# A graph-attention kernel: smaller scratch buffers, a carry read where the matmul left it, and the table's first half written in three pieces

## The chip, the cores and the metric

The kernel runs on one core of one Trainium2 chip. The metric is the device time of one execution in microseconds (us). A core has a matrix engine (PE, with its weight loads shown as PEld), a vector engine (DVE), a scalar engine (ACT), a general engine (POOL) and an engine that only issues transfers and waits (SP). Each runs its own instructions in order. They meet through semaphores. Transfers are issued from the queues of SP, ACT and POOL and are carried out by 16 DMA engines that all queues share, in packets. Matmuls write to PSUM, of which one tile in this kernel is a bank of 512 fp32 columns on 128 partitions; DVE and ACT read PSUM and SBUF.

## What is computed

32 graphs, each `x[b]` of 512 channels by 1024 nodes, pass through two layers. Cut to what matters (the weights `wm`, `support` and `kernel` are all `adj`):

```python
# layer 0: attention over the 1024 nodes of a graph
q = einsum('c,bcn->bn', wq, x);  k = einsum('c,bcn->bn', wk, x)
scores = q[:, None, :] + k[:, :, None]                  # row m, column n
scores = where(scores > 0, scores, 0.01 * scores)
att = softmax(scores, axis=-1)
agg = einsum('bcn,bmn->bcm', x, att)
x = layernorm(x + relu(einsum('oc,bcm->bom', adj, agg) + bm[:, None]))
# layer 1
x = layernorm(x + einsum('bnf,nm->bmf', x, adj * adj) + bias)
```

`layernorm` is over the 1024 nodes, with variance plus 1e-5 and no scale or shift.

The kernel never forms the 1024 x 1024 attention. With the nodes sorted by `q` from the largest down, the nodes of a row `m` with a positive score are the first `of[m]` of the order. Their weights are exp(q) times a factor of the row; those of the others are exp(0.01 q) times another. So a running sum from the top ("up") and one from the bottom ("down") of weighted rows `z = adj x`, kept for every place of the order, hold everything: row `m` reads one line of a table, scales its two halves and adds them.

## The kernel before, in words

All inputs and products are fp32. A batch is one graph. Its stages are small Python functions, each of which issues the instructions of one step; a dictionary `ops` gives each a short word. Three lists of such words, written out in full, `head` (line 827), `loop` (line 1026) and `tail` (line 1044), say in which order all instructions of all engines are issued. A word `td.-1.0` is the step `td` for the batch before the current one, argument 0. `head` covers the first 15 batches of starts, `loop` is issued for b = 15 to 22, `tail` drains. In the steady state four batches are in work at once: the products and ranks of batch b, the table of b - 1, the attention's result of b - 2, layer 1 of b - 3. As every engine runs in order, a step that waits holds all later words of its own engine.

The steps in the order of one batch, with their words:

- `ld` (line 98) loads `x[b]`, four transfers of 128 partitions x 4 KB. `pa`, `pc`, `co`, `cc` (lines 234 to 264) compute q and k; `pc` copies from PSUM to the tile `part`. `qw` and `ro` (lines 266 to 276) write q to DRAM and read it back on all partitions into the tile `qb`.
- `rk` (line 294) ranks the nodes on DVE, `ct` (line 311) counts on ACT; both write a throw-away tile.
- `z`, `zU` and their like compute `z` on PE; `zc` and others copy it to `zt`, which has 514 columns (`ZR`): 512 of `z`, a one, and minus q. `sc` (line 438) scatters its rows to DRAM by rank, with POOL, to `sorted_z`.
- `sl` (line 452) loads the sorted rows in two halves of four rows for each partition into the right side of the tile `tab`, which has 8 rows of 2 x 514 columns on each of the 128 partitions. The pool `one` has one buffer for each tag, so there is one `tab` at a time.
- `se` (line 465) takes the exponentials on ACT. `u` (line 475) makes the 8 running sums from the top within a partition, `d` (line 487) those from the bottom.
- `cu` (line 510) carries the sums of the partitions across partitions, a matmul of a triangle of ones (`before`, whose first column is all ones) with the partitions' totals: output partition p is the sum of the partitions in front of p, and output partition 0 is the total of all. `uc` (line 513) copies it to row 0 of `tab`'s left side with a factor per partition, `inner`, which is 0 on partition 0 and 1 elsewhere. `tu` (line 532) adds that row to rows 1 to 7. `te` (line 536) copies the total to a line of its own, in the buffer of the tag `qb`, and `tl` (line 548) writes that line as row 1024 of the table in DRAM.
- `cd` (line 520) does the same from the other side with `behind`, in two matmuls of 257 columns; `dc` (line 523) copies the carry from PSUM to SBUF, into the buffer of the tag `part`, and `td` (line 540) adds it to the right side of `tab`, four rows at a time.
- `tw` (line 543) writes `tab` to the table in DRAM in two halves, each 128 partitions x 4 rows x 1028 columns: 16,448 contiguous bytes for a partition.
- `tb` and `tp` (lines 278 to 292) fetch the largest q. `g` (line 552) gathers the table's rows by `of`, with POOL; `mw`, `ms`, `mx` (lines 561 to 582) scale and add the halves; `t` (line 596) turns the result on PE; `r` (line 605) adds it to x.
- Then layer 1: `s0`, `rt`, `rce`, `n0` normalise; `t1` to `t4`, `U`, `V`, `Y`, `Z`, `11`, `12`, `21` are its products in a scheme of seven multiplications; `up`, `lr`, `ll` add the parts; `s1`, `ra`, `rb`, `r1`, `n` normalise again, and `st` (line 782) writes the output.

Three tags of the pool `one` matter for the change. `part` holds in turn `part`, DVE's throw-away tile of the ranks, and the down carry. `qb` holds `qb` and the line of the total. `tab` is described above. Where two tiles share a tag, the later one's first write waits for the last use of the earlier one.

PSUM has four single banks that `bank` (line 83) hands out and `release` (line 92) takes back; the dictionary `over` says at which word. The two banks of the down carry come back at `dc`.

## Time and profile before

| | |
|---|---|
| median of 3 runs | 1946.24 us (1945.54 to 1951.74) |
| the profiled execution's own time | 1946.45 us |
| its span, first to last instruction | 1944.7 us |
| mean granted PE clock | 0.991 |
| chain that ended last | PE 72%, DMA 8%, DVE 6%, ACT 5%, issue 2% |
| DMA, mean over the span | 287 GB/s; 558.55 MB moved |

Busy time is what an engine spent in instructions; the rest it waited or had nothing to issue. A group's row gives the line, the engine, the operation, output and inputs, shapes, the count, then busy us and mean ns of one, then the idle time of the engine before them with what ended it. A row of waits reads: engine, line, what it waited for, us in total, times, the longest. "SPq" is SP issuing a transfer; the time it shows is that of issuing, not of the transfer. A DMA queue's line gives packets, MB and the packets' time as a share of 16 engines over the span; q1 is SP's queue, q0 POOL's, q10 ACT's.

The times of one period of the steady part can be read from a batch to the next: the first halves of the table go out at 895.0, 952.6, 1010.2, 1067.7 and 1125.4 us.

### The profile page before, as it was taken

The numbers are of one execution on the slowest core, as the hardware profiler recorded it, in microseconds if no ns is written. First come the engines' busy times: TensorE is split into PE (matmuls) and PEld (weight loads), VectorE is DVE, ScalarE is ACT, GpSimd is POOL, SyncE is SP. The second block draws the span as 40 slices with busy tenths as digits, with TensorE's granted clock in tenths as the row PEclk, the third lists the DMA queues.
The fourth block names the chain that finished last, engine by engine and source line by source line (L and its number), as shares of the span: only waits on it lengthen the run. The fifth ranks groups of instructions, "written<-read, shape, count | busy, mean of one in ns | idle before, by whom it ended". The sixth has DMA issues, their size and how long they took to land.

```text
span 1944.7 us, 23294 instructions
## 1 busy us (share of the span) xinstructions
PE 1871.7 (96%) x6947; PEld 1059.4 (54%) x6949; DVE 1699.4 (87%) x2732; ACT 1543.5 (79%) x2791; POOL 863.2 (44%) x1074
## 2 busy tenths in 40 slices
PE   7997999999999999999999999999999999998897
PEld 3653565555555545556555556555565555554343
DVE  5887899999898989989999988998898999988983
ACT  3556878988888878888888888888887888877896
POOL 4243444455444445444445544445444345445340
PEclk9998999999999999999999999999999999999999
DMA  6467888777878777878787888777788677787762
GB/s 247 165 245 287 309 321 321 267 303 286 335 304 300 285 295 282 327 306 311 288 312 282 304 308 306 299 291 283 291 312 330 270 301 280 298 321 302 277 250 86
DMA packets 147577, 558.55 MB, mean 287 GB/s; under 512 B 19662, under 2 KB 19802, under 8 KB 139260
## 3 DMA queue, kind: packets, MB, share of 16 engines
q1 hardware_dynamic: 90080, 354.92, 48.4%
q0 software_dynamic: 57344, 202.15, 27.4%
q8 instruction: 55, 0.90, 0.2%
q14 instruction: 70, 0.57, 0.1%
q10 hardware_dynamic: 28, 0.01, 0.0%
HBM read 287.59 MB, written 269.42 MB: 286 GB/s over the span
## 4 chain that ended last, share of the span: by engine, by line
PE 72%; DMA 8%; DVE 6%; ACT 5%; issue 2%; POOL 1%; SPq 0%; another core or an unknown queue 0%; DVEq 0%; POOLq 0%; ACTq 0%
PE z_ps L339 17%; PE sum_ps L656 17%; PE pair_ps L656 10%; PE z_sum_ps L383 8%; PE z_pair_ps L383 6%; PE pair_ps L708 5%; PE agg_ps L600 4%; DMA tab<-sorted_z 3%; DMA table<-tab 2%; PE qk_ps L240 2%; DMA x<-in_x_dram 1%; DVE tab L530 1%; PE carry_ps_False L501 1%; DMA got<-table,of 1%; PE carry_ps_True L501 1%
## 5 line engine op out<-in xcount | busy, mean ns | idle before, releaser
L556 POOL DMA_INDIRECT got<-table,of x256 | 294.9, 1152 | 536.2 <-DVE junk_v L301 169.9
L339 PE MATMUL z_ps<-adj_t,x 128*128 128x512 f32 x1088 | 487.8, 596 | 5.8 <-ACT part L248 2.7
L444 POOL DMA_INDIRECT sorted_z<-zt,to x256 | 298.5, 1166 | 212.2 <-ACT zt L345 70.5
L301 DVE SCALAR_TENSOR_TENSOR junk_v<-qb,qkc,tie 128x1024 uint8<-128x1024 f32 x256 | 328.8, 1284 | 18.6 <-DMA qb<-q_row 14.7
L339 PEld LDWEIGHTS z_ps<-adj_t,x 128*128 128x128 f32 x1088 | 203.2, 191 | 231.6 <-issue 217.9
L316 ACT ACTIVATE junk_s<-qb,qkc 128x1024 uint8<-128x1024 f32 x256 | 293.5, 1147 | 34.8 <-DMA qb<-q_row 26.4
L656 PE MATMUL sum_ps<-zt,S 128*128 128x512 f32 x512 | 238.0, 596 | 3.3 <-ACT g L700 2.0
L483 DVE SCALAR_TENSOR_TENSOR tab<-tab,ac 128x514 f32<-128x514 f32 x224 | 168.6, 753 | 42.1 <-ACT tab L479 16.5
L576 ACT ACTIVATE got<-got,bd 128x512 f32<-128x512 f32 x256 | 175.2, 718 | 22.9 <-DVE bd L571 16.1
L581 DVE SCALAR_TENSOR_TENSOR got<-got,bd 128x512 f32<-128x512 f32 x256 | 184.6, 745 | 5.9 <-ACT got L576 4.6
L609 DVE SCALAR_TENSOR_TENSOR x<-agg_ps,small,x 128x1024 f32<-128x1024 f32 x128 | 162.6, 1280 | 21.7 <-PE agg_ps L600 21.3
L591 ACT ACTIVATE junk<-g,tv 128x1024 uint8<-128x1024 f32 x128 | 146.6, 1146 | 42.7 <-DVE g L728 31.7
L493 DVE SCALAR_TENSOR_TENSOR tab<-tab,ac 128x513 f32<-128x513 f32 x224 | 167.4, 747 | 3.8 <-ACT junk_s L316 1.4
L759 POOL TENSOR_SCALAR tv<-tv 128x1 f32<-128x1 f32 x124 | 48.8, 393 | 274.1 <-ACT junk L591 267.1
L656 PEld LDWEIGHTS sum_ps<-zt,S 128*128 128x128 f32 x512 | 96.9, 191 | 123.9 <-issue 108.4
L591 ACT ACTIVATE junk<-x,tv 128x1024 uint8<-128x1024 f32 x128 | 146.8, 1147 | 16.6 <-DVE x L609 13.0
L780 ACT ACTIVATE g<-g,nb,tv 128x1024 f32<-128x1024 f32 x124 | 152.3, 1237 | 7.6 <-POOL nb L770 7.6
L530 DVE TENSOR_TENSOR tab<-tab,carry 128x2052 f32<-128x2052 f32 x64 | 145.1, 2290 | 5.3 <-ACT carry L508 5.3
L627 ACT ACTIVATE x<-x,tv 128x1024 f32<-128x1024 f32 x128 | 140.9, 1141 | 0.3
L600 PEld LDWEIGHTS agg_ps<-ident,got 128*128 128x128 f32 x1024 | 116.2, 141 | 34.8 <-issue 22.0
L600 PE MATMUL agg_ps<-ident,got 128*128 128x128 f32 x1024 | 129.7, 274 | 2.6 <-DVE got L581 1.0
L530 DVE TENSOR_TENSOR tab<-tab 128x1539 f32<-128x1539 f32 (+1 forms) x64 | 129.3, 2023 | 0.6 <-ACT tab L516 0.5
(134 smaller groups left out, 3251.2 us busy)
## 6 DMA issues: line engine op xcount, KB each, us to landing
table<-tab SPq DMA_DIRECT2D x64, 2056.0 KB
tab<-sorted_z SPq DMA_DIRECT2D x64, 1028.0 KB
x<-in_x_dram SPq DMA_DIRECT2D x128, 512.0 KB
out_dram<-g SPq DMA_DIRECT2D x128, 512.0 KB
qb<-q_row SPq DMA_DIRECT2D x32, 512.0 KB
sorted_z<-zt,to POOLq DMA_INDIRECT x256
got<-table,of POOLq DMA_INDIRECT x256
adj_in<-in_adj_dram SPq DMA_DIRECT2D x1, 1024.0 KB
```

The costliest lines, as they stand in the source:

```text
L301: nc.vector.scalar_tensor_tensor(s.junk, s.qb, s.q[:, j : j + 1], tie[:, at : at + N], ALU.subtract, ALU.is_gt, accum_out=s.rank[:, j : j ...
L316: nc.scalar.activation(junk, s.qb, AF.Sign, bias=s.k[:, j : j + 1], accum_out=s.sign[:, j : j + 1])
L339: nc.tensor.matmul(s.z[j], xt[:, c, j * P : (j + 1) * P], adj_t[:, c, :], start=(c == 0), stop=(c == CT - 1),)
L383: nc.tensor.matmul(ps, a[:, i, k * P : (k + 1) * P], v[:, i, :], start=start and i == 0 and (k == 0 or bank == 1), stop=(i == 1), skip_gro ...
L444: nc.gpsimd.indirect_dma_start(out=sorted_z[b % 2][:, :], out_offset=bass.IndirectOffsetOnAxis(ap=s.to[:, j : j + 1], axis=0), in_=zt[:, j ...
L530: nc.vector.tensor_tensor(v, v, c, ALU.add)
L556: nc.gpsimd.indirect_dma_start(out=s.got[:, j, :], out_offset=None, in_=table[b % 2][:, :], in_offset=bass.IndirectOffsetOnAxis(ap=s.of[:, ...
L576: nc.scalar.activation(down, down, AF.Copy, scale=s.bd[:, 1, j : j + 1])
L581: nc.vector.scalar_tensor_tensor(up, up, s.bd[:, 0, j : j + 1], down, ALU.mult, ALU.add)
L591: nc.scalar.activation(junk, t, AF.Square, bias=v[0][:, i : i + 1], scale=-float(N), accum_out=v[1][:, i : i + 1],)
L600: nc.tensor.matmul(s.agg[o][:, j * P : (j + 1) * P], s.got[:, j, o * P : (o + 1) * P], ident, is_transpose=True, start=(j % 4 == 0), stop= ...
L656: nc.tensor.matmul(ps, a[:, k, g * P : (g + 1) * P], v[:, k, :], start=False, stop=(k == 1), skip_group_check=True,)
```

## The change

It has five parts.

- The tag `part` shrinks from 514 to 256 columns and holds only `part`; DVE's throw-away tile gets a tag of its own; the line of the total and the carry's copy are gone.
- The down carry stays in PSUM. `cd` makes it in matmuls of 512 and 2 columns, `dc` is gone, and `td` adds it from there: column 512 for all eight rows at once (in the first `td`), columns 0 to 511 for four rows at a time. The two banks come back at the second `td`.
- `uc` copies without the factor `inner`, so that row 0 of `tab`'s left side holds the total on partition 0. `te` is gone, and `tl` writes row 1024 of the table from there. `tu` is as it was, and so adds the total to rows 1 to 7 of partition 0 too.
- The table's row 0 must have zeros on the left: they are written once at the start, and `tw`'s first half leaves them out, so that it is three transfers: partitions 1 to 127; rows 1 to 3 of partition 0; and the right side of row 0.
- All three order lists are new. The loop's words are the same but for `te` and `dc`; 62 of its 196 words stand elsewhere in the order, mostly by a few places. On SP, `tl` moves behind a store and `qw`; on PE, `cd` moves behind `co` and one `t`.

```diff
-    rows = one.tile([P, ZR], F32, tag="part", name="rows")[0 : 3 * CT, 0:P]
+    rows = one.tile([P, Q], F32, tag="part", name="rows")[0 : 3 * CT, 0:P]
...
-    spare, inner = small[0:1, 9:10], small[:, 10:11]
+    spare = small[0:1, 9:10]
...
-    nc.vector.tensor_scalar(inner, ident[:, 0:1], -1.0, 1.0, ALU.mult, ALU.add)
...
     for t in table:
         nc.scalar.dma_start(out=t[N : N + 1, ZR:], in_=zero)
+        nc.scalar.dma_start(out=t[0:1, 0:ZR], in_=zero)
...
-        s.part = one.tile([P, ZR], F32, tag="part", name=f"part_{b}")[:, 0:Q]
+        s.part = one.tile([P, Q], F32, tag="part", name=f"part_{b}")
...
-            s.junk = one.tile([P, 4 * ZR], U8, tag="part", name=f"junk_v_{b}")[:, 0:N]
+            s.junk = one.tile([P, N], U8, tag="junk_v", name=f"junk_v_{b}")
...
     def carry_up_copy(b):
         half = ZR // 2
         for h, t in enumerate(st[b].cup):
-            nc.scalar.activation(
-                st[b].tab[:, 0, h * half : (h + 1) * half], t, AF.Copy, scale=inner
-            )
+            nc.scalar.copy(st[b].tab[:, 0, h * half : (h + 1) * half], t)
 
     def carry_down(b):
-        st[b].cdown = carry(b, behind, st[b].zs[:, 0, :])
-
-    def carry_down_copy(b):
-        st[b].carry = one.tile([P, ZR], F32, tag="part", name=f"carry_{b}")
-        carry_copy(st[b].cdown, st[b].carry)
+        s, v = st[b], st[b].zs[:, 0, :]
+        s.cdown = []
+        for lo, hi in ((0, C), (C, ZR)):
+            t = bank(f"carry_ps_{b}_{lo}", f"carry.{b}.False", whole=False)[:, 0 : hi - lo]
+            nc.tensor.matmul(t, behind, v[:, lo:hi], start=True, stop=True)
+            s.cdown.append(t)
 
     def spread_carry(v, c):
-        n = v.shape[1]
-        c = c[:, 0:D].rearrange("p (o c) -> p o c", o=1).broadcast_to([P, n, D])
+        n, w = v.shape[1], v.shape[2]
+        c = c[:, 0:w].rearrange("p (o c) -> p o c", o=1).broadcast_to([P, n, w])
         nc.vector.tensor_tensor(v, v, c, ALU.add)
...
-    def table_up_end(b):
-        st[b].end = one.tile([P, N], F32, tag="qb", name=f"total_{b}")[0:1, 0:ZR]
-        carry_copy([t[0:1, :] for t in st[b].cup], st[b].end)
-
     def table_down(b, h):
-        spread_carry(st[b].zs[:, 4 * h : 4 * h + 4, 0:D], st[b].carry)
+        s = st[b]
+        if s.carried is None:
+            s.carried = True
+            spread_carry(s.zs[:, :, C:D], s.cdown[1])
+        spread_carry(s.zs[:, 4 * h : 4 * h + 4, 0:C], s.cdown[0])
 
     def table_write(b, h):
         rows = table[b % 2][0:N, :].rearrange("(p j) c -> p j c", j=NT)
         at = slice(4 * h, 4 * h + 4)
-        nc.sync.dma_start(out=rows[:, at, :], in_=st[b].tab[:, at, :])
+        v = st[b].tab
+        if h:
+            nc.sync.dma_start(out=rows[:, at, :], in_=v[:, at, :])
+            return
+        nc.sync.dma_start(out=rows[1:P, at, :], in_=v[1:P, at, :])
+        nc.sync.dma_start(out=rows[0:1, 1:4, :], in_=v[0:1, 1:4, :])
+        nc.sync.dma_start(out=rows[0:1, 0, ZR : 2 * ZR], in_=v[0:1, 0, ZR : 2 * ZR])
 
     def table_last(b):
-        nc.sync.dma_start(out=table[b % 2][N : N + 1, 0:ZR], in_=st[b].end)
+        nc.sync.dma_start(out=table[b % 2][N : N + 1, 0:ZR], in_=st[b].tab[0:1, 0, 0:ZR])
...
-                due[key] = due.get(key, 2 if key.endswith("True") else 1) - 1
+                due[key] = due.get(key, 2 if key.endswith("False") else 1) - 1
```

Of the new lists, the part of `loop` from the last sums to the table's writes:

```diff
-    ls.-3.0 ls.-3.1 d.-1.0 s1.-3.3 tu.-1.0 z.1.2 te.-1 ra.-3.3 s1.-3.2 tl.-1 mx.-2.0 st.-3.1
-    rb.-3.3 tu.-1.1 pc.1 n.-3.0 qw.1 r1.-3.3 t.-2.2 st.-3.0 zc.1.2 ro.1 cd.-1 ra.-3.2 r.-2.2
-    n.-3.3 rb.-3.2 co.1 t.-2.1 r1.-3.2 dc.-1 cc.1 ce.0 st.-3.3 n.-3.2 t.-2.3 tb.0 r.-2.1 z.1.3
-    st.-3.2 td.-1.0 s0.-2.1 ct.1.7 td.-1.1 tw.-1.0
+    ls.-3.0 ls.-3.1 d.-1.0 uc.-1 st.-3.1 s1.-3.3 tu.-1.0 z.1.2 s1.-3.2 ra.-3.3 mx.-2.0 rb.-3.3
+    pc.1 tu.-1.1 n.-3.0 qw.1 r1.-3.3 tl.-1 t.-2.2 zc.1.2 st.-3.0 ro.1 co.1 r.-2.2 t.-2.1
+    ra.-3.2 n.-3.3 rb.-3.2 cd.-1 cc.1 r1.-3.2 ce.0 r.-2.1 n.-3.2 t.-2.3 st.-3.3 tb.0 z.1.3
+    td.-1.0 s0.-2.1 st.-3.2 ct.1.7 td.-1.1 tw.-1.0
```

## The prediction

> **What bounds the kernel now.** I read the page's busy line first, then one period of the steady part, cut at the events around the table.

> ```profile
> span 1944.7 us, 23294 instructions
> ## 1 busy us (share of the span) xinstructions
> PE 1871.7 (96%) x6947; PEld 1059.4 (54%) x6949; DVE 1699.4 (87%) x2732; ACT 1543.5 (79%) x2791; POOL 863.2 (44%) x1074
> ```

> PE leaves 1944.7 - 1871.7 = 73 us, and none of it in the period below. The next view is the timeline of SP, which issues the transfers (start, time of issuing, line, transfer, count):

> ```profile
> 1010.17 2.54 SPq L546 DMA_DIRECT2D table<-tab  x2
> 1021.85 0.92 SPq L463 DMA_DIRECT2D tab<-sorted_z  x2
> 1048.19 1.77 SPq L101 DMA_DIRECT2D x<-in_x_dram  x4
> ...
> 1067.74 2.53 SPq L546 DMA_DIRECT2D table<-tab  x2
> ```

> The two halves of the table go out (L546), the same tile `tab` is reloaded for the next batch (L463) once they have left it, and 57.57 us after one write comes the next. The first exponential on the reload (L468 on ACT) starts at 1029.72. Those three points cut the period; the view of stretches gives each engine's busy time in them:

> ```profile
> core 0: us, PE busy (x) PEld busy (x) DVE busy (x) ACT busy (x) POOL busy (x), PEclk, DMA share, GB/s
> 1010.20:1021.90 11.70, 11.70 (x42) 7.10 (x41) 11.63 (x20) 10.10 (x20) 0.00 (x0) 1.00 0.86 365
> 1021.90:1029.70 7.80, 7.80 (x37) 6.84 (x36) 6.67 (x12) 5.83 (x8) 5.89 (x5) 1.00 0.87 312
> 1029.70:1067.70 38.00, 38.00 (x142) 19.26 (x141) 34.40 (x56) 32.22 (x61) 22.00 (x29) 1.00 0.77 281
> ```

> PE has no gap, so it is the bound; but a loop of events through `tab` (write, reload, exponentials, sums, write) fills the same period with almost no slack. SP's waits say so:

> ```profile
> SPq L463 <- DMA table<-tab: 242.7, 32, 12.0
> SPq L549 <- ACT total L508: 182.0, 21, 30.9
> ```

> Every one of the 32 reloads waits for the table's transfer, 7.6 us each. Whatever lengthens that transfer by more than a few us lengthens every batch. So I looked at its packets. The tile's 64 half writes are 8,192 packets of 16,448 bytes (one row of partition each), median 616 ns, from 611; 10 to 90 in 100 lie at 613 to 636. One half is 128 packets over 16 engines, 8 x 0.616 = 4.93 us; both halves, 9.9 us, took 10.07 to 11.2 us from first to last packet, so an engine sends them one after another.

> How many engines does a transfer get? The page counts packets by queue, and the small queue of ACT can be counted out whole:

> ```profile
> q1 hardware_dynamic: 90080, 354.92, 48.4%
> q0 software_dynamic: 57344, 202.15, 27.4%
> ...
> q10 hardware_dynamic: 28, 0.01, 0.0%
> ```

> ```profile
> table<-zero ACTq DMA_DIRECT2D x2, 2.0 KB
> rows<-in_L_gnn_wq_dram ACTq DMA_DIRECT2D x1, 2.0 KB
> rows<-in_L_gnn_wk_dram ACTq DMA_DIRECT2D x1, 2.0 KB
> rows<-in_L_gnn_bm_dram ACTq DMA_DIRECT2D x1, 2.0 KB
> ```

> q10 carried three loads of four rows and two writes of one row. The trace has 12 data packets of 512 bytes, 2 of 2,056 and 14 of 4 bytes: the last are closing packets, four for each four-row load (12) and one for each one-row write (2). SP's queue q1 closes the same way: its closing packets are 7,360, which is 450 transfers of 128 rows x 16, plus 32 of four rows x 4, plus 32 of one row x 1. So the row count sets the engines, in equal shares: 128 rows 16 engines, 4 rows 4, 1 row 1.

> **The change, part by part.**

> *The first half's write* (`table_write`, h = 0) becomes three transfers: partitions 1 to 127 (127 x 16,448 bytes), rows 1 to 3 of partition 0 (12,336 bytes), and the right half of its row 0 (2,056). No row of the trace has 127 rows. Lower bound: 16 engines with unequal shares, 8 x 0.616 = 4.9 us, as now. Upper bound: equal shares only. 127 has no divisor up to 16 but 1, so one engine sends 127 x 0.616 = 78.2 us. I take the upper value, because every transfer of the trace has equal shares, and a four-row one stays on 4 engines with 12 idle; nothing evens shares out.

> [...]

> Now the loop again, on the engine that has it all. 78.2 (127 rows), 12,336/16,448 x 0.616 = 0.46, a 2,056-byte packet 0.085, and behind them in the same queue the second half's 8 packets, 4.93: 83.7 us. The shortest stretch from first write to reload in the trace is 11.4 us for 9.86 us of packets, so 1.5 us for start and landing: 85.2 us instead of 12.7 (394.0 us over the 31 stretches between batches). That is 31 x 85.2 - 394 = +2,247 us. The last batch's gathers wait for its table as well: 85.2 - 11.5 = +74.

> What is queued behind the wait: on SP the next x load, total, stores and q row; POOL's gathers wait for the same landing, ahead of the next scatters in its list; ACT stops at the exponentials, with a `norm0`, `u`'s scale and all PSUM copies behind them; DVE at the second `u`; PE, after `U` of the first half, at products of rows that ACT has not normalised. Within some 22 us of the write all stand. What each did meanwhile is saved once: reload to exponentials is 203.5 us over 31 (6.6 each), partly ACT's own lateness; the shortest are 5.2 to 5.5, so 5.4 x 31 = 167, -36 us. Exponentials to the next write (1,166 us over 31, 38 each) I keep: DVE is busy 34.4 of 38.0, in order, most of it behind the reload. It could shrink by 5 us (DVE without gaps, less `T1`, done in the wait), or grow: after PE gaps of 4 to 7 us the profile's clock stands at 0.5 for 3.4 or 6.8 us, so up to 3.4 us of PE a batch after a gap this long.

> *Copies off ACT.* The 64 down copies go (21.3 us busy), the 64 of the totals (20.0), and the 64 scaled copies of 467 ns become plain ones, 369 ns in the same shape: 64 x 0.098 = 6.3. Together 47.6 us, 1.5 a batch. ACT is idle 57.5 - 48.15 = 9.4 us of the period above, so this is worth nothing: PE's work covers it now, the wait after; with neither cover it would be 1.5 us a batch.

> *The carry read in PSUM.* DVE's two additions of 2,052 columns (2,290 ns) become two of 2,048 and one of 8 (an 8-column operation takes 169): +0.16 x 32 = 5 us, inside DVE's 3.6 us of gaps a batch. The rows for the source:

> ```profile
> L643 DVE TENSOR_TENSOR zt<-x 128x1024 f32<-128x1024 f32 x32 | 39.1, 1221 | 1.1 <-ACT x L627 0.9
> L426 DVE TENSOR_TENSOR zt<-z_pair_ps,zt 128x1024 f32<-128x1024 f32 x30 | 36.6, 1219 | 6.7 <-issue 3.7 <-PE z_pair_ps L383 2.9
> ```

> With one operand in PSUM 1,219 ns, with both in SBUF 1,221: no price. [...]

> Two PSUM banks stay held until the second addition instead of the copies, some 5.6 us longer (1064.2 to 1069.8 in this period); if a later product wants them, PE waits for DVE, 0 to 5 us.

> *PE.* The carry matmuls become 512 and 2 columns instead of 257 and 257. The columns stay 514, but a weight load (191 ns) no longer hides behind a two-column pass: 0 to 2 x 0.191 = 0.4 us a batch, 0 to 12 us in all; free under the wait.

> *Buffers and lists.* `part` no longer waits for carry and ranks (ACT waited 4.0 us for that), `qb` not for the total (2.7). `tl` moves on SP behind one store and the q row write; it no longer waits for the copies (182 us of SP's waiting, none seen by PE). In the steady list 62 of 196 words stand elsewhere, by a few places. At set-up two 2 KB writes come, one tiny DVE operation goes. All this lies between the 73 us that PE has to give and a few us of new waits; I take 0.

> Sum against the profiled execution (1946.45 us around its span): 1946.45 + 2,247 + 74 - 36 = 4,231, so **4,230 us**; the shown runs' median, 1946.24, is the same to 0.01%. Its own range: 31 x 5 = 155 less, or 31 x 3.4 = 105 (clock), 31 x 2.4 = 74 (reload as late as the 7.8 above) and 35 (packets at their mean of 624) more: 4,075 to 4,445.

> **Rivals.**

> 1. *The 127 rows are spread over all 16 engines*. Then PE remains the bound, and what is left is the head and tail, where the carry is on the path: from its matmul to the addition 3.3 us, of which the copies 0.6 and the wait for them go, some 1.5 us in four or five batches, -7, less buffer waits of 4.0 and 2.7; against it up to 12 us of weight loads. About 1,943, between 1,933 and 1,958: not slower. It decides from about 11 engines up, where the write is at most 12 packets and the reload's 1 to 2 us of slack hold it. For it: the same bytes in 128 rows do so now. Against: equal shares everywhere.

> 2. *One engine, but other work overlaps better, and only that engine's load bounds.* Its packets: (48.4% + 27.4%) of 1944.7 = 1,474 us, less its 8-packet shares of the first halves (32 x 4.93 = 158), plus 32 x 78.8 = 2,520: 3,837, and some 100 at the ends where it has no table to send: 3,930. Against: one `tab` tile, so reload and transfer can't overlap.

> 3. *One engine, and the stretch behind the wait grows*, since gathers, reload, scatters, x load and stores all start at once and share that engine, whose remaining 41 us a batch must fit in about 44: +5 to 8 us a batch, 4,390 to 4,480. For it: DMA share 0.77 to 0.87 in those stretches today.

> **How the numbers follow.** Forecast 0.74; rival 1 0.05; rival 2 0.07; rival 3 0.14. What a measurement can tell here is about 0.3%. Rival 1 is faster 0.02, same 0.02, slower 0.01; all else is slower: 0.02, 0.02, 0.96. The range leaves out rival 1 and part of rival 2, and takes in the forecast's own range and rival 3: 3,980 to 4,480.

> **What would show it.** Right: closing packets falling by 15 for each first-half write and a single DMA engine busy (mean share near 1/16, about 27 GB/s) for some 80 us a batch; reload about 85 us after the write; all engines idle meanwhile; PE's clock at 0.5 after it. Wrong: table packets ending 5 us after the first, a period of 57 us. The forecast falls if rows aren't shared equally.

## The result, and the profile after

| | before | after |
|---|---|---|
| median, us | 1947.15 (4 runs, 1945.54 to 1951.74) | 4344.73 (4 runs, 4341.93 to 4349.22) |
| ratio | 1 | 2.2307, 95% interval 2.2263 to 2.2351 |
| span of the profiled execution, us | 1944.7 | 4344.7 |
| mean granted PE clock | 0.991 | 0.727 |

The changed kernel takes 2.23 times as long. One run further below, of the last version, took 2481.34 us at a granted clock of 0.75 in place of 0.99; no comparison here counts it. The page of the changed kernel, with the lines for busy time, for SP's queue q1 and for the chain that ended last:

```profile
span 4344.7 us, 23347 instructions
...
PE 1957.2 (45%) x6952; PEld 1085.2 (25%) x6952; DVE 1703.4 (39%) x2763; ACT 1511.0 (35%) x2663; POOL 829.0 (19%) x1069
...
q1 hardware_dynamic: 89696, 354.86, 21.7%
...
DMA table<-tab 26%; SPq L550 21%; PE sum_ps L661 7%; SPq L551 6%; PE pair_ps L661 4%; DMA tab<-sorted_z 4%; PE z_ps L339 4%; DMA out_dram<-g 3%; DMA top<-sorted_z 3%; DVE tab L529 2%; PE pair_ps L713 1%; PE z_sum_ps L383 1%; DVE x L614 1%; PE qk_ps L240 1%
```

The work is the same: PE is busy 1957 us instead of 1872, DVE 1703 instead of 1699. Only the span has grown, and the chain says through what: 53% of it lie on the write of the table, the transfer itself (26%) and SP standing in the issue of it (L550, L551, 27%), where the kernel before had 2% on that transfer. No engine is the bound any more. q1 moved the same 355 MB with 384 packets less: 32 data packets more, since each first half is now 127 + 1 + 1 instead of 128, and 416 packets of 4 bytes fewer (11,040 instead of 11,456). 4,096 of these are data in both kernels, the others close a transfer. 416 is 32 x 13, and the 13 can be counted out: the old first half closed with 16 packets, the new three transfers close with one each.

One period in the middle, SP's timeline (start, time of issuing, line, transfer, count):

```profile
2215.58 0.24 SPq L549 DMA_DIRECT2D table<-tab  x1
2215.87 37.18 SPq L550 DMA_DIRECT2D table<-tab  x1
2253.10 0.73 SPq L551 DMA_DIRECT2D table<-tab  x1
2253.93 1.21 SPq L547 DMA_DIRECT2D table<-tab  x1
2302.78 0.93 SPq L463 DMA_DIRECT2D tab<-sorted_z  x2
2327.66 1.78 SPq L101 DMA_DIRECT2D x<-in_x_dram  x4
```

L549 sends the 127 rows, L550 and L551 the rest of partition 0, L547 the second half. The reload (L463) comes 87.2 us after the first write, where it took 11.7 us in the period shown for the kernel before. Over all 31 batches the mean from the first write of the table to the reload is 88.1 us, against 12.71. (The expectations below have 88.0 and, for one run, 15.05: for one batch, in which the second half goes out first, they count from the first half, some 4 us later.) The same period cut into stretches, busy time of each engine, clock, DMA share:

```profile
core 0: us, PE busy (x) PEld busy (x) DVE busy (x) ACT busy (x) POOL busy (x), PEclk, DMA share, GB/s
2215.60:2237.00 21.40, 20.53 (x81) 14.27 (x80) 18.47 (x32) 16.70 (x28) 0.00 (x0) 1.00 0.11 45
2237.00:2253.00 16.00, 3.54 (x11) 1.65 (x9) 1.98 (x2) 0.05 (x1) 0.00 (x0) 0.73 0.06 27
2253.00:2262.00 9.00, 0.00 (x0) 0.00 (x0) 0.00 (x0) 0.00 (x0) 0.00 (x0) 0.50 0.60 238
2262.00:2297.00 35.00, 0.00 (x0) 0.00 (x0) 0.00 (x0) 0.00 (x0) 0.00 (x0) 0.50 0.06 27
2297.00:2302.40 5.40, 0.00 (x0) 0.00 (x0) 0.00 (x0) 0.00 (x0) 0.00 (x0) 0.50 0.06 25
2302.80:2308.00 5.20, 0.00 (x0) 0.00 (x0) 0.00 (x0) 0.00 (x0) 3.57 (x4) 0.50 0.78 265
2308.00:2347.00 39.00, 36.28 (x130) 17.63 (x131) 32.62 (x54) 30.99 (x56) 21.28 (x30) 0.94 0.78 295
```

A DMA share of 0.06 is one engine of sixteen, and its packets, 16,448 bytes in 0.613 us each in the stretch from 2262, make 26.8 GB/s, the 27 of the table. The compute engines have done nearly all that they can 21 us after the write, and from 2253 to the reload all four stand. At 2253 the second half is issued: fifteen engines send their 8 packets at once (0.60), and the sixteenth still has the 127 rows in front of it. By the packets' records it ends these at 2296.7 and its own 8 packets of the second half at 2302.2. Then the reload starts, and everything runs at the old pace again (0.78, 295 GB/s) until the next write.

Who waited, in us in total, times and the longest:

```profile
POOL got L561 <- DMA table<-tab: 2367.9, 26, 97.1
ACT ac L468 <- DMA tab<-sorted_z: 2130.3, 57, 85.0
DVE tab L483 <- ACT tab L479: 1682.8, 26, 75.5
...
PE pair_ps L713 <- ACT x L632: 627.6, 10, 70.4
```

All four waits are the same standstill seen from four engines. POOL names it directly (the table's transfer); ACT names the reload behind it, DVE names ACT, and PE names ACT's normalised rows. Adding these up would count the same standstill four times.

### The profile page after: what moved, and what is told of

Its sections match the earlier page's. It is cut to its first block, busy times and chain, and to the rows that moved or that the text cites. A ratio compares the mean times of both kernels' runs of the same rounds, so it can differ in the third digit from the quotient of the medians.

```text
span 4344.7 us, 23347 instructions
## 1 busy us (share of the span) xinstructions
PE 1957.2 (45%) x6952; PEld 1085.2 (25%) x6952; DVE 1703.4 (39%) x2763; ACT 1511.0 (35%) x2663; POOL 829.0 (19%) x1069
## 3 DMA queue, kind: packets, MB, share of 16 engines
q0 software_dynamic: 57344, 202.15, 12.2%
## 4 chain that ended last, share of the span: by engine, by line
DMA 38%; SPq 28%; PE 21%; DVE 4%; another core or an unknown queue 4%; ACT 2%; issue 1%; POOL 1%; POOLq 0%; ACTq 0%; DVEq 0%
DMA table<-tab 26%; SPq L550 21%; PE sum_ps L661 7%; SPq L551 6%; PE pair_ps L661 4%; DMA tab<-sorted_z 4%; PE z_ps L339 4%; DMA out_dram<-g 3%; DMA top<-sorted_z 3%; DVE tab L529 2%; PE pair_ps L713 1%; PE z_sum_ps L383 1%; DVE x L614 1%; PE qk_ps L240 1%
## 5 line engine op out<-in xcount | busy, mean ns | idle before, releaser
L561 POOL DMA_INDIRECT got<-table,of x256 | 265.5, 1037 | 2867.6 <-DMA table<-tab 2367.9
L468 ACT ACTIVATE ac<-tab,top 128x4 f32<-128x4 f32 x64 | 19.1, 299 | 2130.3 <-DMA tab<-sorted_z 2130.3
L713 PE MATMUL pair_ps<-x,adj 128*128 128x512 f32 x256 | 150.0, 723 | 922.8 <-ACT x L632 627.6
L339 PE MATMUL z_ps<-adj_t,x 128*128 128x512 f32 x1088 | 489.7, 596 | 10.7 <-DVE tab L529 10.1
L661 PE MATMUL sum_ps<-zt,S 128*128 128x512 f32 x512 | 247.5, 617 | 439.8 <-ACT g L699 296.1
L713 PEld LDWEIGHTS pair_ps<-x,adj 128*128 128x128 f32 x256 | 58.0, 235 | 1002.5 <-ACT x L632 637.6
L661 PE MATMUL sum_ps<-x,adj 128*128 128x512 f32 x256 | 133.0, 645 | 302.9 <-ACT sum_ps L674 222.2
L383 PE MATMUL z_sum_ps<-R,x_sums 128*128 128x256 f32 x480 | 124.2, 405 | 291.4 <-DVE x_sums L373 146.4
L581 ACT ACTIVATE got<-got,bd 128x512 f32<-128x512 f32 x256 | 174.0, 719 | 42.5 <-DVE bd L576 34.8
L383 PEld LDWEIGHTS z_sum_ps<-R,x_sums 128*128 128x128 f32 x480 | 96.6, 204 | 320.0 <-issue 301.8
```

The source lines that it names most:

```text
L339: nc.tensor.matmul(s.z[j], xt[:, c, j * P : (j + 1) * P], adj_t[:, c, :], start=(c == 0), stop=(c == CT - 1),)
L383: nc.tensor.matmul(ps, a[:, i, k * P : (k + 1) * P], v[:, i, :], start=start and i == 0 and (k == 0 or bank == 1), stop=(i == 1), skip_gro ...
L561: nc.gpsimd.indirect_dma_start(out=s.got[:, j, :], out_offset=None, in_=table[b % 2][:, :], in_offset=bass.IndirectOffsetOnAxis(ap=s.of[:, ...
L661: nc.tensor.matmul(ps, a[:, k, g * P : (g + 1) * P], v[:, k, :], start=False, stop=(k == 1), skip_group_check=True,)
L713: nc.tensor.matmul(pair(b, g)[:, 0:H], A12[:, k, g * P : (g + 1) * P], quarters(b)[2][:, k, :], start=(k == 0), stop=(k == 1),)
```

## The experiments

Nine kernels, in three groups; the runs of each group share the chip and the runs of the kernel before. In the expectations A is the theory on record: a transfer's rows go to the engines in equal shares, so 127 rows go to one. The first group asks what it is about the write that costs the time. The trace names no engines. I count them by the closing packets of SP's queue, taken as one for each engine that a transfer uses: a first half closes with 16 in the kernel before, where the first 128 packets of a write had ended 5.1 to 6.3 us after the start of the first, and the 127 rows close with one and took 79.96 us in the period shown. For one first half they are 33 with 112 and 15 (16 + 15, and 1 + 1 for the two small transfers), 17 with 126 and 1 (14 + 1 + 1 + 1), 9 with 122 and 5 (2 + 5 + 1 + 1), 16 with 101 and 26 (1 + 13 + 1 + 1), 63 by rows (16 + 16 + 16 + 15) and 2 in the kernel before split 127 and 1. All are what equal shares give.

### The first half in 112 and 15 partitions

```diff
-        nc.sync.dma_start(out=rows[1:P, at, :], in_=v[1:P, at, :])
+        nc.sync.dma_start(out=rows[1:113, at, :], in_=v[1:113, at, :])
+        nc.sync.dma_start(out=rows[113:128, at, :], in_=v[113:128, at, :])
```

> The changed kernel, but partitions 1 to 127 of the first half go out as 112 rows and 15 rows, two transfers in place of one. A, the row count sets the engines in equal shares: 112 rows on 16 engines, 7 packets of 0.616 us each, 15 rows on 15, one packet; the first half is back to some 5 us, write to reload to 12 to 14 us, the time to 1,945 us (1,935 to 1,965). B, it is the start at partition 1 that puts a transfer on one engine: 112 x 0.62 = 69 us and 15 more, about as slow as the changed kernel, 4,345. C, it is the number of transfers or the new lists: 4,345 or more, since there is one transfer more.

Measured: 1991.54 us (6 runs, 1989.37 to 2007.63), ratio 1.0259 (1.0233 to 1.0285). One more transfer of the same bytes, from the same partition on, with the same order lists, and 2,353 of the 2,398 us are gone. So neither the start at partition 1, nor the number of transfers, nor the new order is what costs the time; the number of rows in one transfer is. 47 us stay, and A had allowed at most 1,965 us. Part is in the write: the mean from write to reload is 15.18 us over the 31 batches, 12.71 before. Many of the 16,448-byte packets are slower: 886 of 8,160 took over 1 us, the longest 3.4; in the kernel before it was 26 of 8,192, and 9 of 10 took at most 636 ns. 340 of the slow ones start in the first 5 us after the write, 451 between 5 and 8 us. In one period (write at 1026.9) 11 of the 23 that started between 1032.3 and 1033.5 took 1.2 to 2.3 us, the others 613 ns or little more. By equal shares each engine has 7 rows of the 112 ahead of it. 7 x 0.616 = 4.3 us, behind a first packet 1.2 us after the write (2216.8 after 2215.6 in the changed kernel's period), make 1032.4, so by this estimate that is when the 15 rows of neighbouring partitions are sent. These rows may slow one another, which no run shows apart from the rest; that can't be the whole reason, since 340 slow packets start before them, and the next run has slow packets without such a group. The other part of the 47 us is found below.

### 126 and 1

```diff
+        nc.sync.dma_start(out=rows[1:127, at, :], in_=v[1:127, at, :])
+        nc.sync.dma_start(out=rows[127:128, at, :], in_=v[127:128, at, :])
```

> The changed kernel with 126 rows from partition 1 in one transfer and partition 127 in another. A: 126 = 14 x 9, so 14 engines with 9 packets, 5.5 us, and one packet more on the first engine: 1,950 us (1,935 to 1,985). B (start at partition 1): 126 x 0.62 = 78 us on one engine, 4,345. C: 4,345.

Measured: 2001.41 us (4 runs, 1989.05 to 2006.71), ratio 1.027 (1.0245 to 1.0294); write to reload 15.45 us. One row fewer in the big transfer takes the mean from 88.1 to 15.45. There is no gradual dependence on size, as there would be with a cost for bytes or for partitions. The time is above the 1,985 us that A allowed, and again packets are slow: 509 of 8,160 took over 1 us, the longest 2.4. What slows them in these two versions stays open. It goes with the split by partitions: with all 128 rows in one transfer (below) it is 35 of 8,192.

### 122 and 5

```diff
+        nc.sync.dma_start(out=rows[1:123, at, :], in_=v[1:123, at, :])
+        nc.sync.dma_start(out=rows[123:128, at, :], in_=v[123:128, at, :])
```

> The changed kernel with 122 rows in one transfer and 5 in another: a dose. A: 122 = 2 x 61, two engines with 61 packets of 0.62, 37.8 us, and 5 rows on 5 engines; with the second half behind it 43.9 us, plus 1.5 to 2, so 45.5 us from write to reload in place of the measured 88.0: 4,345 - 32 x 42.5 = 2,985 us (2,900 to 3,080). SP's issue of the following transfer should not be held if what holds it is some 64 packets outstanding on one engine, since only 61 are. B and C: 4,345.

Measured: 3072.37 us (2 runs, 3070.57 and 3074.18), ratio 1.5798 (1.577 to 1.5825); write to reload 48.3 us. 122 is 2 x 61 with 61 prime, and the time lies where two engines with 61 rows each put it: 48.3 is about midway between 88.1 (one engine) and 12.7 (sixteen). Of the theories on record only equal shares explain this run beside the last two: 122 rows are slow, 126 and 112 are not.

### The kernel before, with only its first half split 127 and 1

```diff
+        nc.sync.dma_start(out=rows[0:127, at, :], in_=v[0:127, at, :])
+        nc.sync.dma_start(out=rows[127:P, at, :], in_=v[127:P, at, :])
```

> The kernel before, with nothing changed but that the first half goes out as partitions 0 to 126 in one transfer and partition 127 in another; lists, buffers and carry are the old ones. A: 127 rows on one engine again, 80 us; 31 x (87.5 - 12.7) = 2,319, less 36, plus 75 for the last batch: 4,300 us (4,230 to 4,400). B (start at partition 1): no change, 1,946. C (lists, buffers or three transfers): within some us of 1,946.

Measured: 4352.04 us (4350.49 and 4353.59), ratio 2.2378 (2.2339 to 2.2416). Nothing else of the change is in this kernel, its order lists are the old ones, and it starts at partition 0. The split alone makes a loss of the same size. SP's timeline in it shows the same issue that takes long:

```profile
2219.20 0.25 SPq L550 DMA_DIRECT2D table<-tab  x1
2219.50 36.52 SPq L551 DMA_DIRECT2D table<-tab  x1
2256.06 1.25 SPq L548 DMA_DIRECT2D table<-tab  x1
2306.03 0.93 SPq L463 DMA_DIRECT2D tab<-sorted_z  x2
```

The second group asks two things: what is left of the change if the write is cheap, and how the held issue depends on the row count.

### The rows of all partitions, by rows

```diff
-        nc.sync.dma_start(out=rows[1:P, at, :], in_=v[1:P, at, :])
-        nc.sync.dma_start(out=rows[0:1, 1:4, :], in_=v[0:1, 1:4, :])
-        nc.sync.dma_start(out=rows[0:1, 0, ZR : 2 * ZR], in_=v[0:1, 0, ZR : 2 * ZR])
+        nc.sync.dma_start(out=rows[:, 1:4, :], in_=v[:, 1:4, :])
+        nc.sync.dma_start(out=rows[:, 0, ZR : 2 * ZR], in_=v[:, 0, ZR : 2 * ZR])
+        nc.sync.dma_start(out=rows[1:113, 0, 0:ZR], in_=v[1:113, 0, 0:ZR])
+        nc.sync.dma_start(out=rows[113:P, 0, 0:ZR], in_=v[113:P, 0, 0:ZR])
```

> The changed kernel with its first half cut by rows of a partition and not by partitions: rows 1 to 3 of all 128, the right side of row 0 of all 128, and the left side of row 0 (2,056 bytes) as 112 and 15 partitions. 8 x 0.462 + 8 x 0.085 + 8 x 0.085 = 5.1 us an engine, four transfers as with 112 and 15. P, fifteen whole rows of neighbouring partitions sent at once slow each other (their packets took 1 to 2.6 us in place of 0.61): here nothing large is sent from few partitions, so write to reload 13 us in place of 15.05, and 1,945 us (1,935 to 1,955). N, four more transfers to issue cost it: 15 us and 1,990 as before. L, lists and carry cost it: 1,985 or so whatever the writes do.

Measured: 1959.22 us (5 runs, 1956.56 to 1961.31), ratio 1.0075 (1.0061 to 1.0089). Write to reload is 13.37 us, near P's 13, and the slow packets are gone: 32 of the 4,096 packets of 16,448 bytes took over 1 us, and 1 of the 4,096 of 12,336 bytes. The table gets the same lines as from the changed kernel (in both, its lines 1 to 7 are left with the total added on the left, which the factor `inner` kept out before), and only the left sides of row 0, 127 pieces of 2,056 bytes, go in odd groups. The time stays 15 us above the kernel before, a third of what 112 and 15 whole partitions do. It fits none of the three ranges: P had at most 1,955 us, N and L some 1,985 to 1,990.

### The first half in one transfer

```diff
-        nc.sync.dma_start(out=rows[1:P, at, :], in_=v[1:P, at, :])
-        nc.sync.dma_start(out=rows[0:1, 1:4, :], in_=v[0:1, 1:4, :])
-        nc.sync.dma_start(out=rows[0:1, 0, ZR : 2 * ZR], in_=v[0:1, 0, ZR : 2 * ZR])
+        nc.sync.dma_start(out=rows[:, at, :], in_=v[:, at, :])
```

> The changed kernel with its first half in one transfer of 128 rows, as before the change; row 0 of the table then holds the total on the left where zeros belong. All the rest of the change alone: P or N: 1,943 us (1,933 to 1,955), write to reload 12.7 us. L: 1,985 or so, with write to reload at 12.7 and the loss in the stretch from the exponentials to the write.

Measured: 1955.96 us (5 runs, 1953.07 to 1959.35), ratio 1.0063 (1.0049 to 1.0076). Write to reload is 12.89 us, against 12.71 before: the transfers are those of the kernel before. The version leaves out the zeros on the left of the table's row 0. By difference 35 us of the 112-and-15 version came from its write, then, and some 12 us belong to the other parts of the change; P and N had at most 1,955 us in all. PE's waits name them; PE's timeline shows one (start, duration, line, tiles, count, and in brackets the idle time ahead and what ended it):

```profile
PE z_ps L339 <- DVE tab L529: 10.1, 12, 1.1
...
PE z_sum_ps L383 <- DVE tab L529: 2.7, 3, 1.5
```

```profile
951.30 1.14 PE L523 MATMUL carry_ps<-tab,behind 128*128 128x512 f32 x4
952.30 1.07 PE L603 MATMUL agg_ps<-ident,got 128*128 128x128 f32 x8
953.21 3.60 PE L339 MATMUL z_ps<-adj_t,x 128*128 128x512 f32 x8
957.68 3.67 PE L339 MATMUL z_ps<-adj_t,x 128*128 128x512 f32 x8 [0.87 <-DVE tab L529]
```

PE makes the carry at 951.3 and comes back at 957.7 to write a product of `z` into a bank that the carry still holds. DVE's addition, which reads the carry there, isn't done. 10.1 + 2.7 = 12.8 us of such waits, none of which the kernel before has: it copied the carry out at once.

### 101 and 26

```diff
+        nc.sync.dma_start(out=rows[1:102, at, :], in_=v[1:102, at, :])
+        nc.sync.dma_start(out=rows[102:128, at, :], in_=v[102:128, at, :])
```

> The changed kernel with 101 rows (a prime) in one transfer and 26 in another. Equal shares: 101 x 0.63 = 63.6 us on one engine, 26 on 13 engines, 2 packets each, 1.2; 0.55 and 4.9 behind: 70.3 plus 2 = 72.3 us from write to reload, so 4,345 - 32 x 15.7 = 3,843 us (3,750 to 3,930). SP's next issue: if one engine takes some 64 to 70 packets ahead, held about (101 - 67) x 0.63 = 21 us; if it is held for a fixed share of the transfer (35 of 80), 28 us; not at all if the hold belongs to 127 rows.

Measured: 3868.31 us (one run), beside 1944.19 for the kernel before; write to reload 73.3 us. 101 is prime like 127, and the transfer again goes at one engine's rate: 101 x 0.616 = 62.2 us of the 73.3, where sixteen engines with at most 7 packets each would take 4.3. This and the run with 122 rows answer the question about the issue. Their timelines, first the one with 101 rows, then that with 122:

```profile
2087.55 0.24 SPq L549 DMA_DIRECT2D table<-tab  x1
2087.83 18.59 SPq L550 DMA_DIRECT2D table<-tab  x1
```

```profile
1576.32 0.24 SPq L549 DMA_DIRECT2D table<-tab  x1
1576.62 0.51 SPq L550 DMA_DIRECT2D table<-tab  x1
```

The issue behind 127 rows on one engine takes 35.2 us (median), behind 101 rows 19.0, behind 61 rows for each of two engines 0.4: there it is not held. The 19.0 us are near the 21 of a fixed number of packets and far from the 28 of a fixed share. In a few batches (6 of 32 with 127 rows, 3 with 101) the first issue behind passes and the next one is held.

The third group tests the waits for banks.

### The same two, with any bank for that product

`bank` prefers a bank whose flag `filled` agrees with what is asked for, and takes the first idle one otherwise. In the steady list the step `z.1` asks two words after the carry's banks came back in the order, and the preference picks one of these. One other bank is idle too, and has been for longer, but its flag doesn't agree. The edit lets this step take the first idle bank:

```diff
         want = [i for i in idle if filled[i] == keep] or idle
+        if key.startswith("z.") and key.endswith(".1"):
+            want = idle
```

On the version by rows:

> The kernel cut by rows (e5), with one line more in the allocator of PSUM banks: the product z of block 1 takes the bank that has been idle longest. Until now it took a bank of the down carry, just given back at the second addition, while two others were idle, and PE stood 12 times 0.8 to 1.1 us for that addition (10.1 us in e5 and e6). If the held banks are what the rest of the change costs: 1,959 less 10 = 1,949 us, two zeroing matmuls (some 0.4 us each) included. If the lists or the new matmul shape cost it: 1,957 to 1,960, the wait turning up elsewhere.

On the version in one transfer:

> The same line in the kernel with the whole first half in one transfer (e6), row 0 of the table left wrong as there. Banks: 1,956 less 10 = 1,946 us, level with the kernel before. Lists or shape: 1,954 to 1,957.

Measured: by rows 1944.70 us (12 runs, 1941.08 to 1948.77), ratio 1.0006 (0.9994 to 1.0018); in one transfer 1943.96 us (median of 12 runs, 11 of them 1939.59 to 1946.98), ratio 1.0000 (0.9987 to 1.0012). Against the runs of the kernel before beside each, the excess falls from 15.0 to 1.5 us and from 11.8 to 0.8. PE's waits in the second, where the lines stand two further down:

```profile
PE z_sum_ps L385 <- DVE tab L531: 3.1, 3, 1.5
...
PE z_ps L341 <- DVE tab L531: 0.3, 1, 0.3
```

The 10.1 us of waits for the carry's bank at `z_ps` are 0.3 now; those at `z_sum_ps`, where the edit changes nothing, stay at 3. The page of this version:

```profile
span 1944.1 us, 23207 instructions
...
PE 1871.8 (96%) x6952; PEld 1053.9 (54%) x6954; DVE 1701.1 (88%) x2763; ACT 1506.6 (77%) x2663; POOL 852.3 (44%) x1069
```

PE is busy 1871.8 us of 1944.1; it was 1871.7 of 1944.7 before. With the write and the banks out of the way, the rest of the change (buffers, copies off ACT, the carry in PSUM, the new lists) is together worth nothing that can be measured: the two intervals leave it 0.2% either way. Parts of it that cancel one another were not taken apart. No version here beats the kernel before.

Not tried: the new small buffers alone in the kernel before. They have 256 columns, and the carry's copy, which shares the tag there, has 514.

## Why the prediction held, point by point

The time was 4,344.7 us against a forecast of 4,230 with a range of 3,980 to 4,480. The mechanism was the one named, and the sum is short by 115 us (4,344.7 us of span, against 4,229.7 from the terms for the profiled execution):

| stretch, us | forecast | measured | difference |
|---|---|---|---|
| up to the first write | 91.8 | 84.0 | -8 |
| write to reload, 31 | 31 x 85.2 = 2,641 | 2,732.3 (88.1 each, 86.7 to 91.2) | +91 |
| reload to exponentials, 31 | 31 x 5.4 = 167 | 172.0 | +5 |
| exponentials to next write, 31 | 1,166 | 1,190.7 | +25 |
| behind the last write | 89.4 + 74 = 163 | 165.7 | +2 |

- *Equal shares, so one engine.* Right, and shown in three ways: by the closing packets (one for the 127 rows; 13 fewer for a first half and not the 15 foretold, since the two small transfers add one each), by the 0.06 DMA share, and by the times and closing packets of the runs with 101, 122 and 126 rows.
- *78.2 us for the 127 rows.* This is the term that was mis-sized most. In the period shown it is 79.96 us from the first packet's start to the last one's end, and 80.8 us in the mean of the batches in which the first half goes out first: 2.6 us of the missing 2.9. The packets' records show where. As long as this engine sends alone, its packets start 0.618 us apart before the second half and 0.616 behind it (means over the batches), as in the prediction. While the second half's packets are under way on the other fifteen engines (2253 to 2263 in the period shown) 12 of its packets took 9.6 us in place of 7.3, and single packets on record there took 1.2 to 1.4 us. The prediction had the second half behind the 127 rows on their own engine, but not beside them on the others. Why the packets slow one another is open. The other 0.3 us lie at the ends: 1.8 us for start and landing in place of 1.5.
- *The work behind the wait stands within 22 us.* Right but for a few instructions: 3.5 us of PE and 2.0 of DVE came later than 21.4 us.
- *Exponentials to the next write kept at 38 us, the clock as a bound on top.* The average grew from 37.6 to 38.4. The table of stretches shows a clock of 0.50 at the restart and 0.94 over the rest. PE's busy time rose by 85 us over the whole kernel with all but the same instructions, and 25 of it at most lengthened this stretch; what hides the rest was not tried. The value I took, 0, was too low, and the bound of 105 held it.
- *Copies off ACT are worth nothing.* Right. Summed over its groups, ACT's busy time is 47.5 us less in the last version than in the kernel before (1,681.6 against 1,729.1; the page, which counts what overlaps once, has 1506.6 against 1543.5), and the kernel's time is the same within 0.1%.
- *The carry in PSUM has no price on DVE.* Right. The groups of the changed kernel, shapes apart:

```profile
L529 DVE TENSOR_TENSOR tab<-tab,carry_ps 128x2048 f32<-128x2048 f32 x64 | 144.3, 2280 | 0.0
L529 DVE TENSOR_TENSOR tab<-tab 128x2052 f32<-128x2052 f32 x32 | 73.3, 2291 | 0.1
...
L529 DVE TENSOR_TENSOR tab<-tab,carry_ps 128x8 f32<-128x8 f32 x32 | 5.3, 166 | 5.6 <-PE carry_ps L523 5.6
```

  2,048 columns with the carry in PSUM take 2,280 ns, 2,052 columns all in SBUF 2,291: the same per column.
- *Banks held longer, 0 to 5 us.* This term was mis-sized: 12.8 us of waits, and 11 to 13.5 us of time once it is undone. The prediction took the hold of 5.6 us and asked whether a product would want the bank. It didn't follow the rule in `bank` through the list, which would have shown that it hands out just these banks. The changed kernel has the same waits, 10.1 and 3.0 us, all of them 2 to 5 us behind the write, in a stretch that ends with all engines standing for the table: there they cost nothing that shows. With a cheap write they are all that is left.
- *The two-column matmuls, 0 to 12 us.* Not seen; the 12 us were an estimate from the 191 ns of a weight load. There are 64 x 209 ns in place of half of the 257-column passes, and PE's busy time is 1871.8 us in the last version against 1871.7 before.
- *Lists, 0.* Right for the steady part, by the last version. The first write came 8 us earlier in the changed kernel, and in all versions with the new lists (83 to 84 us).
- *A reading.* The 242.7 us that reloads wait for the table belong to 31 reloads and not 32 (7.8 us each): the first batch's has no write in front of it. Nothing in the sum rests on it.

The rivals. *Spread over 16 engines* (about 1,943) would have been right for a version whose large transfers have rows that divide by 16; the versions in one transfer and by rows show it: 1,944 and 1,945 with the banks mended. *Only the one engine's load bounds* (3,930) falls by the table of stretches: for 35 us only that engine moves anything, so the work doesn't overlap. *The stretch behind the wait grows by 5 to 8 us a batch* (4,390 to 4,480): it grew by 0.8, at a DMA share of 0.78 against 0.77 before.

## What to carry to other kernels

## What the runs showed of the hardware that was not expected

- The issue of a transfer held SP for tens of us when an earlier one had many packets outstanding on one DMA engine: 35 us behind 127 packets, 19 behind 101, none behind 61. At 0.63 us a packet, 35/0.63 = 56 and 19/0.63 = 30 packets had to leave first, so by this estimate about 71 could stand in front: 127 - 56 and 101 - 30 agree. The packets' records say the same: when the issue ended, 67 to 76 of the 127 were left, and 68 to 75 of the 101 (44 in the three batches in which a later issue was held). Here it should have cost little, because the reload waits for the same engine's packets in any case; no run takes the hold away alone. Whether it delays loads that have nothing to do with the table, in another list, was not tried.
- 16,448-byte packets, mostly 0.613 to 0.616 us, slow down when the first half goes out by parts of the partitions: 886 of 8,160 took over 1 us with 112 and 15 rows, 509 with 126 and 1, against 26 of 8,192 before. Cut by rows of all partitions, 32 of 4,096 did. What makes the difference was not tried.
